# Two images take turns in the 256-state scan, and their block products are made source by source

## The chip, the cores and the metric

The kernel runs on one core of a Trainium2 chip, in one launch. The metric is the device time of an execution in microseconds. Everything is 32-bit floating point. The engines are named as the profile names them: PE is TensorE (PEld its weight loads), DVE is VectorE, ACT is ScalarE, POOL is GpSimd, SP is SyncE, which issues the transfers.

## What is computed

The input is four images of 128 channels and 64 x 64 pixels, that is 4096 positions each. A first layer orders 4 x 4 patches by a score, runs a 16-state scan over them and puts the result back. The second layer, where the change lies, has a selective scan with 256 states and then a long convolution. Cut to what matters, for one image (t is 4096 x 128, normalised before each of the two steps; z, gate and weights as in the code):

```python
# 256-state scan: two halves of 128 inner channels, 256 states
xs, z = split(norm(t) @ W_in)
delta, Bv, Cv = xs @ W_delta, xs @ W_B, xs @ W_C
state = exp(delta[i] * A) * state + delta[i] * Bv[i] * xs[i]      # for every position i
y[i] = sum_n state[:, n] * Cv[i, n]
t = t + (y * silu(z)) @ W_out
# spectral step: 16 causal filters phi over the whole length, with weights M for plus and minus,
# four branches over the first 1, 1/2, 1/4, 1/8 of the positions, plus three taps M_u
t = t + sum_k causal_conv(phi[:, k], norm(t)) @ M[k] + ...
```

The convolution is causal: output positions of a block of 1024 need all earlier blocks and the block itself, of which only the lower triangle.

## The kernel before, in words

`layer0_front` and `layer0_scan` do the first layer; the change doesn't touch them. `layer1` does the second, with an order written out by hand: instructions stand on each engine as the program issues them.

**The scan.** An image is cut into eight chunks of 512 positions (`TS`, `NCH`). A part is one chunk of one image; `parts` (L1207) lists the 32 parts, all chunks of image 0, then of image 1, and so on. A part has 256 steps `k`, and each step does one row d of 2 x 512 elements: `fetch` (L1126, eight steps ahead, two rows at once) loads delta to all partitions, `spread` (L1140, POOL, line L1143, four steps ahead) multiplies it with u, `lift` (L1150, ACT, L1152, one step ahead) makes the decay factors, `scan` (L1154, DVE, L1155) runs the recurrence. After eight steps `contract` (L1160) multiplies the states with c on PE (L1172), copies the products out (L1178), writes them to memory and keeps the last state of every row in `last`, which `carry` (L1132, POOL) adds to the next chunk's first column. A single `last` and a single two-column `halo` serve all images, since chunks of an image follow one another.

**Beside the scan.** `beside` runs, in pieces between the steps, `output` of the part just finished (L916: loads of x2 and gate, gating, output product, normalisation, a token tile for the spectral step, the three-tap product at L973, sum, store to x3) and `project` of the part to come (L809). After each second chunk `output` calls `block`, which queues block products of the spectral step.

**The spectral step.** A task is an image `b`, an output block `blk` of 1024 positions (512 even and 512 odd ones, `r`), and a list of source blocks. It runs 2 x 16 x 2 repetitions (r, filter k, side). A repetition makes, for each source, four products of 128 x 128 tokens with 512 columns of a strip of the filter (L1103; where source and block are the same, with 512, 384, 256 and 128 columns), copies the sum out on ACT (L1114), and multiplies it with the filter's weights `pq` into `fin` (L1047). `load` (L1006) issues the transfers of a repetition, `pq` (L1014, four buffers) and `strip` (L1020, three buffers), three queue entries ahead. Images 0 to 2 get one task for each block with all its sources. Image 3 gets tasks for single sources as these come ready; their sums go to memory as `partial` and are added later through an identity product (L1055). `products` yields the columns of each product, and the main loop takes from it as many columns a step as its pace allows: 1.4 x 512 columns for parts below 20, 1.7 x 512 from there (L1275). What is not taken by the last step, and what the last chunk's output still queues, is issued after the loop by `go_on`, until eight calls in a row gave nothing.

Of the kernel before, what the change touches and what calls it, by code (L numbers as in the profile page):

```python
# [701 lines left out]
def layer1_weights(nc, pool, w_in, w_delta, w_b, w_c, w_out, a_t):  # L702
# [3 lines left out]
    wc = pool.tile([128, 2, 256], F32, name="wc")  # L706
    for t, s in ((wbd[:, :, 0:256], w_b), (wbd[:, :, 256:512], w_delta), (wc, w_c)):
        nc.sync.dma_start(t, s.rearrange("(k p) n -> p k n", p=128))
# [4 lines left out]
    return win, wbd, wc, wo, at  # L713
# [3 lines left out]
def layer1(ctx: ExitStack, tc, ident, half, weights, phi, pqd, mud, x, omd, permd, x2, x3, out):  # L717
# [29 lines left out]
    ones = wp.tile([128, 128], F32, name="ones")  # L747
    nc.vector.memset(ones, 1.0)
# [8 lines left out]
    halo = wp.tile([128, 2], F32, name="halo")  # L757
    last = wp.tile([128, 2, 256], F32, name="last")
# [7 lines left out]
    def small():  # L766
        return sm.tile([128, TS], F32, tag="t2", name="t2")
# [31 lines left out]
    def tiles():  # L799
# [5 lines left out]
            big.tile([128, 2, 256], F32, tag="af", name="af"),  # L805
# [3 lines left out]
    def project(b, ch, into):  # L809
# [39 lines left out]
        for j in range(2):  # L849
# [5 lines left out]
            nc.vector.tensor_tensor(u[:, j, :], ps, xs[:, j, :], ALU.mult)  # L855
        for j in range(2):
            yield "mm"
            ps = middle()
            for k in range(2):
                nc.tensor.matmul(ps, wc[:, k, bass.ts(j, 128)], xs[:, k, :], start=k == 0, stop=k == 1)  # L860
# [13 lines left out]
            d0 = sm.tile([128, 128], F32, tag="d0", name="d0", bufs=1)  # L874
            nc.scalar.activation(d0, ident, AF.Copy, scale=dl[:, 0:1])
            yield "mm"
            ps = middle()
            nc.tensor.matmul(ps[:, 0:128], ones, d0, start=True, stop=True)
# [8 lines left out]
    def put_back():  # L887
# [3 lines left out]
        for h in range(2):  # L891
            for oy in range(4):
# [3 lines left out]
                perm = sm.tile([128, 2, 128], F32, tag="mu", name="perm", bufs=1)  # L896
# [19 lines left out]
    def output(b, ch, yt, gate):  # L916
# [32 lines left out]
        if ch % 2 == 0:  # L949
            tokens[b, ch // 2] = sp.tile([128, 2, 4, 128], F32, tag="tok", name="tok", bufs=5)  # L950
# [9 lines left out]
        mu = sm.tile([128, 3, 128], F32, tag="mu", name="mu", bufs=1)  # L960
        nc.sync.dma_start(mu, mud[:, (0, 1, 2, 2, 3, 3, 3, 3)[ch]])
        yield "post"
        ut = sm.tile([128, 2 + TS], F32, tag="ut", name="ut", bufs=1)
        nc.scalar.copy(ut[:, 2:].rearrange("p (a q) -> p q a", q=2), up.rearrange("p (q a) -> p q a", q=2))
        if ch:
            nc.scalar.copy(ut[:, 0:2], halo)
        else:
            nc.scalar.activation(ut[:, 0:2], ident[:, 0:2], AF.Copy, scale=0.0)
        nc.scalar.copy(halo, ut[:, TS:])
# [7 lines left out]
        if ch % 2:  # L977
            block(b, ch // 2)
# [8 lines left out]
    partial = dr.tile([4, 2, 128, TS], F32, name="partial", bufs=1)  # L987

    def block(b, blk):


        if b < NB - 1:
            tasks = [(b, blk, range(blk + 1), False, True)]
        else:
# [5 lines left out]
            )[blk]  # L1000
        for task in tasks:
            queue.extend(
                (task, r, k, side, src) for r in range(2) for k in range(NK) for side in range(2) for src in task[2]
            )

    def load(i):  # L1006
# [3 lines left out]
        (b, blk, sources, _, _), r, k, side, src = queue[i]  # L1010
        if src == sources[0]:
# [11 lines left out]
    def products():  # L1023
# [6 lines left out]
        def finish(item):  # L1030
            nonlocal fin, xo, sofar
            (b, blk, _, partly, full), r, k, side, pq, u = item
# [4 lines left out]
            cost = TS  # L1037
# [8 lines left out]
            for n, (c0, w) in enumerate([(0, 256), (256, 256)] if blk == 0 else [(0, 512)]):  # L1046
# [4 lines left out]
            if partly and (k, side) == (NK - 1, 0):  # L1051
                sofar = sp.tile([128, TS], F32, tag="conved", name="sofar")
                nc.sync.dma_start(sofar, partial[blk, r])
# [3 lines left out]
            if end:  # L1057
                f, o = fin, xo

                def add():  # L1060
# [5 lines left out]
                    else:  # L1066
                        t = sp.tile([128, TS], F32, tag="conved", name="sum")
                        nc.scalar.copy(t, f)  # L1068
                        nc.sync.dma_start(partial[blk, r], t)
# [4 lines left out]
        while True:  # L1074
# [18 lines left out]
            task, r, k, side, src = queue[i]  # L1093
            b, blk, sources = task[:3]
            if src == sources[0]:
# [4 lines left out]
            for j in range(4):  # L1100
# [4 lines left out]
                    start=src == sources[0] and j == 0, stop=src == sources[-1] and j == 3,  # L1105
                )
                if j < 3:
                    yield TS - skip
            i += 1
            if src == sources[-1]:  # L1110
                u = sp.tile([128, TS], F32, tag="conved", name="conved")

                def empty(u=u, ps=ps):
                    nc.scalar.copy(u, ps)  # L1114
# [17 lines left out]
    def carry(ch, d, ready):  # L1132

        af, vf = ready[4:]
        cols = bass.ds(d, 128)
# [24 lines left out]
    def contract(s, c, g, keep):  # L1160
# [20 lines left out]
        def carried():  # L1181
            if keep:
# [190 lines left out]
```

## Time and profile before

| | |
|---|---|
| median of three runs | 21742.6 us (21742.6 to 21744.73) |
| the profiled execution, its own time | 21746.66 us |
| its span, first to last instruction | 21744.9 us |
| granted PE clock, mean | 0.903 |
| PE busy | 17469.3 us (80%) |
| DVE busy | 20628.6 us (95%) |
| ACT busy | 15865.3 us (73%) |
| POOL busy | 20221.1 us (93%) |
| spread, POOL L1143 | 4096 x 4536 ns |
| scan, DVE L1155 | 8192 x 2272 ns |
| transfers | 4245.65 MB, mean 195 GB/s |

Times of instructions come from the one profiled execution. Busy time is a share of the whole span, and says nothing of which stage an engine holds up; for that the span has to be cut into stages. A matmul in 32 bits shows as two passes, so counts of PE in the profile are twice the program's.

### The profile page before, as it was taken

What the parts mean: (1) busy time and instruction counts of PE and PEld (TensorE: products, weight loads), DVE (VectorE), ACT (ScalarE), POOL (GpSimd) and SP (SyncE); (2) the same over time, 40 slices, a digit from 0 to 9 for tenths busy, and PEclk for the clock granted to TensorE, in tenths of its full rate; (3) what the DMA queues carried; (4) which work ended last, traced back from release to release, by engine and by line L of the source; (5) the groups of instructions that cost most, each with busy time, mean ns of one, the idle gap of its engine ahead of it and who ended that gap; (6) DMA issues with size and microseconds to landing.
All of it is one profiled execution on the core that took longest, in us unless ns stands there. A gap on an engine that the chain in (4) does not pass through costs nothing.

```text
span 21744.9 us, 291339 instructions
## 1 busy us (share of the span) xinstructions
PE 17469.3 (80%) x98516; PEld 7646.0 (35%) x98516; DVE 20628.6 (95%) x11808; ACT 15865.3 (73%) x29216; POOL 20221.1 (93%) x5679
## 2 busy tenths in 40 slices
PE   6788854565858888877768888869498899999999
PEld 3344421222323333333323333324143344434344
DVE  6788889999999999999999999999999999999993
ACT  3677767777777777777777777777777777877773
POOL 2677789999999999999999999999999999999993
PEclk7999966776979999998879999979699999999999
DMA  1455544555757777766667777757476777777775
GB/s 68 112 139 141 140 149 151 173 178 163 217 171 219 219 222 220 218 205 196 201 189 218 222 218 220 222 183 231 154 235 216 226 235 235 234 232 231 232 227 150
DMA packets 2420940, 4245.65 MB, mean 195 GB/s; under 512 B 795208, under 2 KB 1255024, under 8 KB 2416368
## 3 DMA queue, kind: packets, MB, share of 16 engines
q1 hardware_dynamic: 2419440, 4227.01, 63.6%
q8 instruction: 776, 12.71, 0.2%
q14 instruction: 724, 5.93, 0.1%
HBM read 3605.76 MB, written 620.24 MB: 194 GB/s over the span
## 4 chain that ended last, share of the span: by engine, by line
DVE 51%; POOL 23%; PE 9%; ACT 8%; issue 6%; DMA 2%; SPq 0%; DVEq 0%; POOLq 0%; ACTq 0%
DVE s L1155 44%; POOL v L1143 22%; ACT da L1152 5%; PE conv L1103 4%; DVE states L513 3%; DVE p L517 1%; PE yp L1172 1%; ACT f L505 1%; PE fin L1047 1%; PE y L529 1%; DMA dlb<-delta 1%; PE mm L422 1%; DMA yd<-ye 1%; PE conv L104 0%; DVE sum L106 0%
## 5 line engine op out<-in xcount | busy, mean ns | idle before, releaser
L1143 POOL TENSOR_TENSOR v<-u,dlb 128x2044 f32<-128x2044 f32 x4096 | 18333.8, 4536 | 68.1 <-DMA dlb<-delta 64.9
L1155 DVE TENSOR_TENSOR_SCAN s<-da,v 128x1024 f32<-128x1024 f32 x8192 | 18130.6, 2272 | 192.7 <-ACT da L1152 91.1
L1152 ACT ACTIVATE da<-dlb,at 128x511 f32<-128x511 f32 x16384 | 11302.4, 690 | 2235.1 <-DVE s L1155 1774.2
L1103 PE MATMUL conv<-strip,tok 128*128 128x512 f32 (+3 forms) x20480 | 8609.0, 550 | 5.9 <-DMA strip<-in_phi 5.8
L1172 PE MATMUL yp<-s,c 128*32 128x256 f32 x65536 | 5030.9, 438 | 3065.5 <-DVE s L1155 1601.6
L1103 PEld LDWEIGHTS conv<-strip,tok 128*128 128x128 f32 x20480 | 3666.5, 191 | 4104.4 <-issue 3705.1
L1172 PEld LDWEIGHTS yp<-s,c 128*32 128x32 f32 x65536 | 1992.5, 121 | 6865.7 <-issue 1822.2
L1147 ACT COPY v<-vf 128x4 f32<-128x4 f32 x4096 | 812.7, 198 | 2234.0 <-DVE s L1155 2228.7
L491 POOL TENSOR_TENSOR v<-dx,bcb 128x1024 f32<-128x1024 f32 x512 | 1207.2, 2358 | 433.6 <-DVE states L513 427.3
L1047 PE MATMUL fin<-conved,pq 128*128 128x512 f32 (+1 forms) x3200 | 1411.8, 536 | 11.1 <-ACT sum L1068 4.1
L513 DVE TENSOR_TENSOR_SCAN states<-f,v 128x1024 f32<-128x1024 f32 x512 | 1175.9, 2297 | 176.1 <-ACT f L505 126.5
L505 ACT ACTIVATE f<-dt,an 128x255 f32<-128x255 f32 x2048 | 973.6, 476 | 420.0 <-DVE states L513 369.2
L1178 ACT COPY ye<-yp 128x512 f32<-128x512 f32 x2048 | 1185.0, 579 | 16.7 <-PE yp L1172 15.4
L529 PE MATMUL y<-p,ident 128*128 128x512 f32 x2048 | 1004.8, 619 | 152.3 <-DVE p L517 147.4
L1114 ACT COPY conved<-conv 128x512 f32<-128x512 f32 x1344 | 778.0, 579 | 327.7 <-PE conv L1103 326.4
L517 DVE TENSOR_TENSOR p<-states,bcb 128x1024 f32<-128x1024 f32 x512 | 627.0, 1225 | 38.2 <-PE y L535 0.4
L529 PEld LDWEIGHTS y<-p,ident 128*128 128x128 f32 x2048 | 368.3, 195 | 684.0 <-issue 356.3
L1047 PEld LDWEIGHTS fin<-conved,pq 128*128 128x128 f32 x3200 | 528.0, 193 | 221.3 <-issue 160.7
L422 PE MATMUL mm<-ow,yg 128*32 128x128 f32 x2048 | 280.5, 296 | 106.8 <-ACT om L426 105.3
L1063 DVE TENSOR_TENSOR xo<-xo,fin 128x512 f32<-128x512 f32 x32 | 21.3, 667 | 306.8 <-PE fin L1055 306.8
L422 PEld LDWEIGHTS mm<-ow,yg 128*32 128x32 f32 x2048 | 235.3, 138 | 212.5 <-ACT om L426 128.4
L356 PE MATMUL mm<-xin,taps 128*128 128x512 f32 x512 | 237.2, 606 | 28.3 <-DVE f L335 14.0
(242 smaller groups left out, 5932.4 us busy)
## 6 DMA issues: line engine op xcount, KB each, us to landing
dlb<-delta SPq DMA_DIRECT2D x4096, 512.0 KB, 4.1
strip<-in_phi SPq DMA_DIRECT2D x1536, 448.0 KB, 4.8
yd<-ye SPq DMA_DIRECT2D x2048, 256.0 KB, 4.1
bcb<-bcd SPq DMA_DIRECT2D x1024, 256.0 KB, 4.2
strip<-in_phi SPq DMA_DIRECT2D x1024, 256.0 KB, 4.4
pq<-pqd SPq DMA_DIRECT2D x1088, 64.0 KB, 3.8
yt<-yd SPq DMA_DIRECT2D x4096, 4.0 KB, 3.4
pq<-pqd SPq DMA_DIRECT2D x256, 128.0 KB, 4.0
```

What stands on the lines that cost most here:

```text
L491: nc.gpsimd.tensor_tensor(v, ready[n][2][:, :, bass.ts(i, SUB)].unsqueeze(1).broadcast_to((128, 2, 2, SUB)), bc[:, 0].unsqueeze(2).broadca ...
L505: nc.scalar.activation(factors[j % 2][:, a, k, 1:], ready[n][1][:, k, SUB * i + 1 : SUB * i + SUB], AF.Exp, scale=an[:, k, 2 * g + a : 2 * ...
L513: nc.vector.tensor_tensor_scan(states.rearrange(flat), factors[j % 2].rearrange(flat), v.rearrange(flat), 0.0, ALU.mult, ALU.add)
L517: nc.vector.tensor_tensor(p, states, bc[:, 1].unsqueeze(2).broadcast_to((128, 2, 2, SUB)), ALU.mult)
L529: nc.tensor.matmul(t.rearrange("p k t -> p (k t)"), ident, p[:, a].rearrange("p k t -> p (k t)"), start=g == 0 and a == 0, stop=False, ski ...
L1047: nc.tensor.matmul(fin[:, bass.ds(c0, w)], pq[:, n, :], u[:, bass.ds(c0, w)], start=begin and n == 0, stop=end and not partly, skip_group_ ...
L1103: nc.tensor.matmul(ps[:, skip:], tok[:, 1 - r if side else r, j, :], strip[:, bass.ds(c0 - lo, TS - skip)], start=src == sources[0] and j ...
L1143: nc.gpsimd.tensor_tensor(v[:, :, :, 1:], ready[0][:, :, 1:].unsqueeze(1).broadcast_to((128, VD, 2, TS - 1)), dl[:, :, 1:].unsqueeze(2).br ...
L1152: nc.scalar.activation(da[:, h, 1:], dl[:, d % VD, 1:], AF.Exp, scale=at[:, h, d : d + 1])
L1155: nc.vector.tensor_tensor_scan(s[:, d % GD].rearrange("p h t -> p (h t)"), da.rearrange("p h t -> p (h t)"), v[:, d % VD].rearrange("p h t ...
L1172: nc.tensor.matmul(yp[i // 2][bass.ts(q, 32), i % 2], c[:, h, t], s[:, :, h, t], start=h == 0, stop=h == 1)
L1178: nc.scalar.copy(ye, yp[j].rearrange("p i d t -> p i t d"))
```

## The change

Images 0 and 1 are done as before. Then `parts` takes chunk 0 of image 2, chunk 0 of image 3, chunk 1 of image 2, and so on to chunk 7 of image 3. For this `last` and `halo` exist twice, chosen by `b % 2`, and so does `partial`.

Both images' block products are now queued source by source, as image 3's were. The last block's own source of image 3 is split in two: after chunk 6 a task with the token groups 0 and 1 (columns 512 and 384), after chunk 7 a task with groups 2 and 3 (columns 256 and 128), whose copies and closing products take only the last 256 columns. A task's sources are now pairs of a source and its groups. The pace is 1.7 x 512 from part 16.

To make room, W_C is no longer kept in the core's memory but loaded by every `project`; the three-tap weights, their input `ut`, the permutation and W_C share the buffers of the small tiles, three in place of two; `af` has one buffer in place of two; there are six token tiles in place of five. The first delta of a chunk is spread over the partitions by a product with a broadcast column in place of a diagonal tile made on ACT. The loop at the end waits for 16 empty calls in place of eight.

```diff
-    halo = wp.tile([128, 2], F32, name="halo")
-    last = wp.tile([128, 2, 256], F32, name="last")
+    halos = [wp.tile([128, 2], F32, name=f"halo{i}") for i in range(2)]
+    lasts = [wp.tile([128, 2, 256], F32, name=f"last{i}") for i in range(2)]
...
-        return sm.tile([128, TS], F32, tag="t2", name="t2")
+        return sm.tile([128, 2 + TS], F32, tag="t2", name="t2", bufs=3)[:, 0:TS]
...
-            big.tile([128, 2, 256], F32, tag="af", name="af"),
+            big.tile([128, 2, 256], F32, tag="af", name="af", bufs=1),
...
+        wcs = small().rearrange("p (k n) -> p k n", k=2)
+        nc.sync.dma_start(wcs, wc)
...
-            d0 = sm.tile([128, 128], F32, tag="d0", name="d0", bufs=1)
-            nc.scalar.activation(d0, ident, AF.Copy, scale=dl[:, 0:1])
...
-            nc.tensor.matmul(ps[:, 0:128], ones, d0, start=True, stop=True)
+            nc.tensor.matmul(ps[:, 0:128], dl[:, 0:1].broadcast_to((128, 128)), ident, start=True, stop=True)
...
-        mu = sm.tile([128, 3, 128], F32, tag="mu", name="mu", bufs=1)
+        mu = small()[:, 0:384].rearrange("p (i c) -> p i c", i=3)
...
-        if ch % 2:
+        if (b, ch) == (NB - 1, NCH - 2):
+            add([(b, 3, [(3, range(2))], True, False)])
+        elif (b, ch) == (NB - 1, NCH - 1):
+            add([(b, 3, [(3, range(2, 4))], True, True)])
+        elif ch % 2:
             block(b, ch // 2)
...
-        if b < NB - 1:
+        if b < NB - 2:
             tasks = [(b, blk, range(blk + 1), False, True)]
...
-            for n, (c0, w) in enumerate([(0, 256), (256, 256)] if blk == 0 else [(0, 512)]):
+            for n, (c0, w) in enumerate([(0, 256), (256, 256)] if blk == 0 else [(first, TS - first)]):
...
-            for j in range(4):
+            for j in js:
...
-                    nc.scalar.copy(u, ps)
+                def empty(u=u, ps=ps, cols=cols):
+                    nc.scalar.copy(u[:, cols], ps[:, cols])
...
-    parts = [(b, ch) for b in range(NB) for ch in range(NCH)]
+    parts = [(b, ch) for b in range(NB - 2) for ch in range(NCH)]
+    parts += [(b, ch) for ch in range(NCH) for b in (NB - 2, NB - 1)]
...
-        pace = 1.4 if n < 5 * NCH // 2 else 1.7
+        pace = 1.4 if n < 2 * NCH else 1.7
...
-    while idle < 8:
+    idle = 0
+    while idle < 16:
         go_on()
```

## The prediction, made before the result

> **What bounds the kernel now.** I read the page first (the 40 slices), then the 256-state scan cut into its 32 equal parts, then the end of the timeline, then the transfers of that end. All sums are made against the profiled execution: span 21744.9 us, time 21746.7 us, about 4 us above the median of 21742.6 us.
>
> The slices of the page:
>
> ```profile
> PE   6788854565858888877768888869498899999999
> DVE  6788889999999999999999999999999999999993
> POOL 2677789999999999999999999999999999999993
> PEclk7999966776979999998879999979699999999999
> ```
>
> From the sixth slice on VectorE and GpSimd are full, and only in the last one do both fall to 3 while TensorE stays at 9. So there are two regimes: a long one set by scan and spread, and a short end that TensorE has alone. The scan runs from 2863.2 to 21376.7 us. Cut into 32 parts of 578.5 us, one chunk of one image each (columns: stretch and its length, then PE, PEld, DVE, ACT, POOL busy with counts, clock, DMA share, GB/s):
>
> ```profile
> core 0: us, PE busy (x) PEld busy (x) DVE busy (x) ACT busy (x) POOL busy (x), PEclk, DMA share, GB/s
> 4598.80:5177.40 578.60, 264.05 (x2136) 105.48 (x2132) 574.00 (x284) 420.53 (x775) 578.29 (x137) 0.62 0.48 151
> 6334.50:6913.00 578.50, 433.68 (x2687) 177.18 (x2678) 571.94 (x282) 428.88 (x793) 576.31 (x136) 0.86 0.65 200
> 17905.40:18484.00 578.60, 554.47 (x3303) 270.22 (x3304) 570.43 (x285) 451.57 (x841) 577.28 (x137) 1.00 0.77 236
> 20219.60:20798.20 578.60, 553.13 (x2992) 219.46 (x2992) 571.70 (x283) 461.48 (x862) 578.29 (x137) 1.00 0.75 232
> ```
>
> GpSimd is busy for 576 to 578 of 578.5 us in each. TensorE between 264 and 554 us, DMA between 48% and 77%: the length of the part doesn't move with either. The end, in the timeline:
>
> ```profile
> 21374.41 2.26 DVE L1155 TENSOR_TENSOR_SCAN s<-da,v 128x1024 f32<-128x1024 f32 x1
> ...
> 21386.32 0.43 SPq L923 DMA_DIRECT2D t<-gate  x1
> ...
> 21390.63 0.69 DVE L930 TENSOR_TENSOR t<-mm,t 128x512 f32<-128x512 f32 x1 [13.96 <-DMA t<-gate]
> ...
> 21741.22 0.34 SPq L1065 DMA_DIRECT2D out<-xo  x1
> ```
>
> The last scan ends at 21376.7 us, the span at 21744.9: **an end of 368.2 us**, in which TensorE is busy for 358 us (the same view over that stretch). Counted in the order of the TensorE queue, behind the last scan's products stand 210,432 columns (393 convolution, 100 closing matmuls and a few others). The steady state of its last task, the first repetition and the start of the second:
>
> ```profile
> 21601.84 2.32 PE L1103 MATMUL conv<-strip,tok 128*128 128x512 f32 x8
> ...
> 21602.03 0.32 SPq L1014 DMA_DIRECT2D pq<-pqd  x1
> ...
> 21602.40 0.42 SPq L1020 DMA_DIRECT2D strip<-in_phi  x1
> ...
> 21603.99 1.02 PE L1047 MATMUL fin<-conved,pq 128*128 128x512 f32 x2
> ...
> 21604.86 2.32 PE L1103 MATMUL conv<-strip,tok 128*128 128x512 f32 x8
> ```
>
> 3.02 us for 512+384+256+128+512 = 1792 columns, 1.685 ns a column, with no hole. 210,432 x 1.685 = 355 us, plus some 13 us of edges, is the end. The transfers in it (21545 to 21745 us; the three columns of the queue are packets, MB, share):
>
> ```profile
> q1 hardware_dynamic: 18539, 22.14, 42.9%
> ...
> strip<-in_phi SPq DMA_DIRECT2D x61, 256.0 KB, 3.5
> pq<-pqd SPq DMA_DIRECT2D x61, 64.0 KB, 1.8
> ```
>
> A strip lands 3.5 us after its issue (3.1 to 4.4), and here that is hidden, since three are in flight and three repetitions last 9 us.
>
> **The change, part by part.**
>
> *The tail's work.* Counted in the order of the changed program, 47,104 columns stand behind the last scan's products: 64 repetitions of 256+128 convolution and 256 closing columns (40,960), 1,024 of partial sums and 5,120 of the chunk's own output. Nothing else is left: the half task queued one part earlier and all of image 2 end 32 steps before the last scan. So 163,328 columns, 275 us at the rate above, leave the end. That would be the gain if TensorE set the new end. It doesn't.
>
> *What is late next: the strips.* A repetition now has 640 columns, 1.08 us, while its two loads are the same (256 KB, of which only 256 of 512 columns are read, and 64 KB). There are three strip buffers; the load for repetition i+2 waits for the closing matmul of i-2, which stands right behind convolution i-1 (its pq load, ahead of it in the same queue, has four buffers). The circle over three repetitions: convolution 384 x 1.685 = 0.65, closing 0.43, 0.19 to the issue of pq and 0.37 more to that of the strip (the fence above), landing 3.5, about 0.1 to start: 5.25 us, 1.75 us each. DMA: 0.33 MB in 1.75 us is 187 GB/s; the row gives 111 GB/s at 42.9%, so some 260 GB/s if full, 1.27 us each: not the bound, but it may stretch the landing to what it is for such strips under load (4.3 us from 10000 to 11000 us): 2.0 us.
>
> *The clock.* The Trainium skill (TensorE: Matmul & The Clock Gate, Part 1: The HAM clock gate) says that the array falls to half rate only after an idle window of about 3.4 us and is else at full rate. Holes of 0.7 us would then cost nothing: 1.75 us. The rows are less kind: the part with TensorE busy for 264 of 578 us was granted 0.62, and that with 434 of 578 us (75%) 0.86; the new tail is busy for 60%. At half rate the 1.08 us double, and it is 6.3/3 = 2.1 us. I take 1.88 us, near the rule but with a little of both losses: 63 x 1.88 = 118 us; ends 110 and 132 (101 if every strip lands in 3.1 us).
>
> *The way from the last scan to the first of these.* Before, the gate lands 13.9 us after the last scan. From there, taking only durations and leaving out the waits behind queued work: gating and transposes 2.6, output product and sum 2.8, transposes, copy, statistics 2.9, GpSimd and normalisation 3.7, flip and copy 2.0, transposes and copy 1.7, the three-tap product 2.9, sum 0.7: 33 us after the scan; then the store's issue and the pq and strip issues (0.8), and a landing of 3.5 to 4: 38 us. In the last part the spectral queue is empty for those 32 steps, so TensorE is cold as in the parts with scan products alone, where the same lines take 3.78 us for 1.88 (L934), 5.1 for 2.8 (L973), 3.64 for 1.93 (each of two groups of L1172): up to 10 us more. I take 44 us.
>
> *Close.* From the start of the last convolution to the end of the span before: 9.5 us (21735.4 to 21744.9); now 1.1 us of convolution and 0.4 of closing less: 8. Between the two halves of the task one sum and a wait for the single accumulator: 2.
>
> New end: 44 + 118 + 2 + 8 = **172 us** against 368: **196 us less**.
>
> *What is added under the scan.* Parts 16 to 31 get 349,184 columns more: 163,328 from the end, and 185,856 new (image 2 by sources closes 320 times more, the split 64 times, 12 more partial sums), 313 us of TensorE. No part's count goes over 237,824 columns; parts 26 to 30 of before held 237,312 to 237,568 and ran their 578.6 us, and the third row above (part 26, 596 matmuls) is as dense in instructions as any new part. So zero, as long as TensorE stays under the part's length; cover gone, it costs what it overruns. ScalarE: some 25 more copies a part, 0.58 us each, 15 us on 462 of 578. DMA: 384 more pq loads of 64 to 128 KB and a weight load of 256 KB each chunk: under 4 MB a part on 134; the parts at 75 to 77% show no loss. From below no gain is possible: GpSimd is full. From above: parts with full TensorE are 1 to 1.5 us longer than light ones (578.7 against 577.2 between scan starts), and 8 parts change sides: at most 10 us. I take 0 and keep 10.
>
> *Waits that are added.* The load of W_C, the taps and the permutation now take turns with the chunk's small tiles (three buffers in place of two); they stand in SP's queue, and behind them are the delta loads that GpSimd waits for. Delta is fetched eight steps ahead and spread four steps later, 9 us, against a landing of 4.6. At each of these places the old tenant's last reader is at least one group of eight steps back (18 us), so 0; a full miss would cost one spread, 4.5 us, a few times. The factor tile with one buffer: its last reader is GpSimd at step 118, the next writer comes near step 200: 0. One small ScalarE instruction per half chunk goes: off the path. States and halos per image: the carried state is now a part old: 0. The ordering of images 0 and 1 is unchanged.
>
> **Rivals.**
> 1. *TensorE sets the new tail.* If strips land early enough, 63 x 1.08 = 68 us: end 38+68+10 = 116, time about 21490 us. For it: the present tail has no hole. Against: three buffers over a landing of at least 3.1 us give 1.6 us.
> 2. *The strips are later or the clock lower, and the scan loses the few us kept above.* 48 + 132 + 4 + 8 = 192, and 10: about 21576 us.
> 3. *Slower: TensorE becomes the bound of parts 16 to 31.* SP's load for a repetition waits for TensorE (166 us of SP waits for the closing matmul already stand in the last six parts), the delta loads stand behind it, GpSimd behind these. It decides from the point at which a part's TensorE work passes 578.5 us; the densest now take 553 to 556. If the new mix took 600, 14 parts would lose 22 us, 301 in all: 21742.6 - 196 + 301 = 21848 us. Against: the same column count with 596 matmuls fitted.
> 4. *Work is left at the end after all.* The count of the program's order excludes it.
>
> **How the numbers follow.** Likeliest: 21742.6 - 196 = 21547 us, its own range 21522 to 21567. Chances: this case 0.79, rival 1 0.06, rival 2 0.10, rival 3 0.03, a loss in the scan that eats most of the gain 0.02. A measurement of this kernel can tell about 0.2%, 43 us, from no change; so faster 0.95, same 0.02, slower 0.03. The range from 21515 to 21583 takes in rival 2 and the earliest landing; rival 1 and the scan's losses stay out.
>
> **What would show it.** After: last scan again at about 21377 us; no part of the scan over 580 us; first convolution of the last task some 44 us later; repetitions of 1.75 to 2.1 us in which TensorE waits for strips, 1.08 if rival 1 holds; clock in the tail between 0.7 and 1; GpSimd waits for delta grown only if rival 3 holds. I am wrong if the scan's end moves by over 10 us, or if the strips' circle isn't what paces the tail.

## The result, and the profile after

The changed kernel takes 21605.9 us, the median of four runs (21600.6 to 21610.8), against 21743.7 us for the kernel before in the same series (21742.6 to 21745.3). The ratio is 0.9936 with a 95% interval of 0.9924 to 0.9947. That is 138 us less where 196 were forecast, and 23 us above the top of the range. The profiled execution of the changed kernel took 21607.9 us, its span 21606.2 us.

The slices of its page (40 equal parts of the span, busy share in tenths):

```profile
PE   6788854564858888886858999599999999999997
...
POOL 2677789999999999999999999999999999999996
```

The last slice is now mostly scan: GpSimd's last digit is 6 where it was 3, and TensorE's is 7, no longer 9. The end has become short, and TensorE doesn't fill it. The next view cuts the changed kernel at the starts of its scans (columns as before: stretch, its length, busy time of each engine with counts, clock, DMA share, GB/s). The rows are parts 3, 26 and 31, the way from the last scan to the last task, and the last task:

```profile
core 0: us, PE busy (x) PEld busy (x) DVE busy (x) ACT busy (x) POOL busy (x), PEclk, DMA share, GB/s
4595.70:5174.00 578.30, 261.99 (x2120) 104.36 (x2120) 573.09 (x283) 418.91 (x771) 577.99 (x137) 0.62 0.47 152
17937.20:18517.90 580.70, 554.51 (x3166) 245.79 (x3170) 573.30 (x284) 447.08 (x831) 580.39 (x137) 1.00 0.75 230
...
20840.30:21432.20 591.90, 519.71 (x3095) 236.93 (x3093) 570.06 (x271) 461.10 (x839) 573.03 (x131) 0.95 0.72 216
21432.20:21472.00 39.80, 20.05 (x92) 8.30 (x92) 3.90 (x12) 5.26 (x13) 1.21 (x2) 0.61 0.12 39
21472.00:21606.20 134.20, 90.95 (x388) 63.92 (x388) 1.38 (x2) 23.81 (x64) 0.00 (x0) 0.94 0.68 171
```

Two things stand here. GpSimd still fills parts 3 and 26, but part 3 lasts 578.3 us where the same chunk of the same image lasted 577.2 before (between the same scan starts), with TensorE at 262 us and the DMA at 47%: a light part, which the new order doesn't touch, has become longer. And in part 31 GpSimd is not full: 573.0 of 591.9 us.

The balance of the two spans, from the starts of the scans in both traces (us):

| | before | after | difference |
|---|---|---|---|
| first scan starts | 2863.2 | 2858.9 | -4.3 |
| parts 0 to 15 (images 0 and 1) | 9255.7 | 9273.8 | +18.1 |
| parts 16 to 30 | 8681.7 | 8707.5 | +25.8 |
| part 31, to the start of its last scan | 573.8 | 589.6 | +15.8 |
| the whole scan, to the last one's end | 18513.5 | 18573.2 | +59.7 |
| end: last scan to end of span | 368.2 | 174.0 | -194.2 |
| span | 21744.9 | 21606.2 | -138.7 |

Where the text gives the length of part 31 it is measured like this, to the start of its last scan, which is 2.3 us short of its end. The end of 174.0 us is 2 us from the forecast of 172. All that is missing was given back under the scan, where the forecast had put nothing.

**The end.** The timeline of the changed kernel from the last scan on (start, duration, engine, line, out<-in, and in brackets the idle time ahead and its releaser):

```profile
21448.09 0.69 DVE L927 TENSOR_TENSOR t<-mm,t 128x512 f32<-128x512 f32 x1 [15.93 <-DMA t<-gate]
...
21450.73 3.78 PE L931 MATMUL mm<-t,wo 128*128 128x512 f32 x4 [0.78 <-DVE t L927]
...
21472.47 0.44 SPq L1027 DMA_DIRECT2D strip<-in_phi  x1
...
21476.52 1.65 PE L1113 MATMUL conv<-strip,tok 128*128 128x256 f32 x4 [5.64 <-DMA strip<-in_phi]
```

The gate lands 15.9 us behind the last scan's end (21432.2), 2 us later than before. The output product takes 3.78 us, as in a light part. The first strip is issued 40.3 us behind the last scan, and the first convolution starts 44.4 us behind it. A repetition in the steady state of the last task, and the start of the next:

```profile
21500.40 0.42 SPq L1027 DMA_DIRECT2D strip<-in_phi  x1
21500.42 0.89 PE L1113 MATMUL conv<-strip,tok 128*128 128x256 f32 x4 [0.42 <-DMA strip<-in_phi]
21501.15 0.60 PE L1055 MATMUL fin<-conved,pq 128*128 128x256 f32 x2
...
21502.14 0.89 PE L1113 MATMUL conv<-strip,tok 128*128 128x256 f32 x4 [0.40 <-DMA strip<-in_phi]
```

Both convolutions wait for their strip; in the old end's steady state none did. Over the whole last task TensorE waits for a strip 48 times in 64 convolutions, 37.9 us in all, and SP in its turn waits 58 times, 60.7 us in all, until a closing matmul (L1055) lets it issue the next `pq` (L1021), with the strip behind it. From the first to the last of the 64 convolutions 122.1 us pass, 1.94 us a repetition. The transfers of that stretch (21480 to 21600 us: the queue's packets, MB and share; then the size of a strip load and the median time from its issue to its landing):

```profile
q1 hardware_dynamic: 17789, 20.86, 68.8%
...
strip<-in_phi SPq DMA_DIRECT2D x60, 256.0 KB, 3.6
```

A strip still lands 3.6 us after its issue, now at 69% of the DMA and not 43%.

**The scan.** The row of the spread on the pages, of the kernel before and then of the changed one (busy time, mean ns of one, idle time ahead of it on its engine and what ended most of that):

```profile
L1143 POOL TENSOR_TENSOR v<-u,dlb 128x2044 f32<-128x2044 f32 x4096 | 18333.8, 4536 | 68.1 <-DMA dlb<-delta 64.9
```

```profile
L1155 POOL TENSOR_TENSOR v<-u,dlb 128x2044 f32<-128x2044 f32 x4096 | 18381.6, 4552 | 78.1 <-DMA dlb<-delta 68.3
```

As many spreads with the same shapes are busy for 47.8 us more, and GpSimd stands idle ahead of them for 10.0 us more: 57.8 of the 59.7 us. Waiting for delta grew by 3.4 us. (Neighbouring spreads overlap by some 60 ns in the records, so 4096 times the mean is more than the busy time; the busy column and the lengths of the parts are what to compare.)

The added idle time comes in the last part: 14.2 us ahead of its spreads, where the last part of the kernel before had none. Its waits of over a microsecond, in the timeline of the changed kernel, hang together:

```profile
20994.76 0.43 SPq L1027 DMA_DIRECT2D strip<-in_phi  x1
...
20999.16 3.26 PE L1113 MATMUL conv<-strip,tok 128*128 128x512 f32 x4 [3.12 <-DMA strip<-in_phi]
...
21002.46 0.59 ACT L1125 COPY conved<-conv 128x512 f32<-128x512 f32 x1 [4.12 <-PE conv L1113]
...
21004.49 4.47 DVE L1167 TENSOR_TENSOR_SCAN s<-da,v 128x1024 f32<-128x1024 f32 x2 [3.51 <-ACT da L1164]
```

A strip is issued at 20994.76 us and lands 4.4 us later (the median of that part is 4.4), and TensorE has waited 3.1 us for it. ScalarE stands at the copy of that convolution, with the decay factors of the scan behind it in its queue, and is 4.1 us late. VectorE waits 3.5 us for the factors. The late convolution is also slow: 3.26 us, where the same products at 20988.75 us took 1.67. The clock granted from 20998.8 to 21002.2 us was 0.50; it fell so after four of the part's waits for strips.

### The profile page after: what moved, and what is told of

It reads as the page before. It is cut to its first block, busy times and chain, and to the rows that moved or that the text cites. A ratio compares the mean times of both kernels' runs of the same rounds, so it can differ in the third digit from the quotient of the medians.

```text
span 21606.2 us, 294251 instructions
## 1 busy us (share of the span) xinstructions
PE 17698.4 (82%) x99308; PEld 7770.7 (36%) x99308; DVE 20631.8 (95%) x11807; ACT 16015.2 (74%) x29548; POOL 20268.9 (94%) x5679
## 4 chain that ended last, share of the span: by engine, by line
DVE 47%; POOL 22%; PE 13%; ACT 8%; issue 6%; DMA 3%; SPq 0%; DVEq 0%; POOLq 0%; ACTq 0%
DVE s L1167 40%; POOL v L1155 21%; PE conv L1113 5%; ACT da L1164 5%; DVE states L513 3%; PE yp L1184 2%; DVE p L517 1%; PE fin L1055 1%; ACT f L505 1%; DMA dlb<-delta 1%; PE y L529 1%; DMA strip<-in_phi 1%; PE mm L422 1%; DMA yd<-ye 0%; PE conv L104 0%
## 5 line engine op out<-in xcount | busy, mean ns | idle before, releaser
L1155 POOL TENSOR_TENSOR v<-u,dlb 128x2044 f32<-128x2044 f32 x4096 | 18381.6, 4552 | 78.1 <-DMA dlb<-delta 68.3
L1184 PE MATMUL yp<-s,c 128*32 128x256 f32 x65536 | 4952.4, 431 | 2709.5 <-DVE s L1167 1432.2
L1055 PE MATMUL fin<-conved,pq 128*128 128x512 f32 (+1 forms) x3968 | 1799.7, 546 | 16.2 <-ACT sum L1076 8.9
L1125 ACT COPY conved<-conv 128x512 f32<-128x512 f32 (+1 forms) x1728 | 986.6, 571 | 213.8 <-PE conv L1113 212.1
L1055 PEld LDWEIGHTS fin<-conved,pq 128*128 128x128 f32 x3968 | 669.8, 194 | 394.8 <-issue 284.0
L356 PE MATMUL mm<-xin,taps 128*128 128x512 f32 x512 | 237.6, 608 | 27.2 <-issue 13.8
L398 POOL TENSOR_TENSOR e<-e,e 128x1024 f32<-128x1024 f32 x32 | 75.1, 2346 | 186.3 <-DMA bcb<-bcd 150.6
```

The source lines that it names most:

```text
L1055: nc.tensor.matmul(fin[:, bass.ds(c0, w)], pq[:, n, :], u[:, bass.ds(c0, w)], start=begin and n == 0, stop=end and not partly, skip_group_ ...
L1125: nc.scalar.copy(u[:, cols], ps[:, cols])
L1155: nc.gpsimd.tensor_tensor(v[:, :, :, 1:], ready[0][:, :, 1:].unsqueeze(1).broadcast_to((128, VD, 2, TS - 1)), dl[:, :, 1:].unsqueeze(2).br ...
L1184: nc.tensor.matmul(yp[i // 2][bass.ts(q, 32), i % 2], c[:, h, t], s[:, :, h, t], start=h == 0, stop=h == 1)
```

## The experiments

The times of a round were taken on one chip with runs of the kernel before beside them. Each kernel below ran once, `a_best` four times. The lengths of parts come from the trace of each run; parts 0 to 15 are those of images 0 and 1, which both kernels order alike.

### Does the absolute place of the tiles slow the spread; what does the last part's pace cost; what paces the tail?

Parts 0 to 15 became longer though nothing in their order changed, so the first theory was the place of tiles in memory: the new memory plan has u start at byte 31072 of a partition and not at 31552. Two kernels shift everything: the kernel before by 32 bytes, the changed one by 480 (u is back at 31552). The rival is contention from new transfers. A third kernel lowers the pace in the last part only, a fourth halves the strip loads in the last task, of which only the columns used are then loaded.

`b_pad32`, the kernel before with

```diff
+    shift = wp.tile([128, 8], F32, name="shift")
+    nc.vector.memset(shift, 0.0)
```

> The kernel before, with one unused tile of 32 bytes a partition ahead of the second layer's tiles, and nothing else: every later tile stands 32 bytes further on. In the changed kernel even the parts of images 0 and 1, whose work is the same, take 1.2 us longer each, and the mean spread went from 4536 to 4552 ns. Theory 'place': that comes from where the tiles stand (u, delta and v change places modulo 64 bytes against each other and the start), so this kernel's parts grow by about 1.2 us each, the spread's mean to about 4550 ns, the time to about 21743 + 38 = 21780 us. Theory 'work': it comes from what the change adds (loads of W_C, shared buffers, more traffic), so this kernel stays at 21743 us and 4536 ns.

Measured: 21748.9 us beside 21750.2; parts 0 to 15 9255.2 us, spread busy 18333.5. Nothing moved.

`a_pad480`, the changed kernel with the same two lines and `[128, 120]`.

> The changed kernel with an unused tile of 480 bytes a partition, which puts u at the very address that it had before, and delta and v at the same place modulo 64 bytes as before. Theory 'place': the spread's mean returns to about 4536 ns, parts 0 to 15 to their lengths before, the time to about 21606 - 38 = 21568 us. Theory 'work': no change, 21600 to 21611 us and 4552 ns.

Measured: 21605.8 us; parts 0 to 15 9275.2 us, spread busy 18380.3. Nothing moved either. A shift of all the layer's tiles together is not the cause, and the theory in this form fell.

`a_pace`, the changed kernel with

```diff
-        pace = 1.4 if n < 2 * NCH else 1.7
+        pace = 1.4 if n < 2 * NCH else 1.7 if n < 31 else 1.55
```

> The changed kernel with a pace of 1.55 x 512 columns a step in place of 1.7 in the last part alone; the queue is then just empty at the last scan. In the changed kernel the last part takes 589.6 us against 573.8 before, with TensorE waiting for strips and ScalarE and VectorE behind it around step 62 to 94. If that is the half task's short repetitions asking for strips faster than SP and three buffers bring them, a lower pace spreads them: the last part at 575 to 580 us, time about 21595 us. If it is something that the pace does not set (the loads of y in the same queue, or the output of the chunk before), the last part stays at 586 to 590 us and the time at 21606 us.

Measured: 21603.9 us. The last part took 577.5 us, 12.1 less than with the change as it was. In this run parts 0 to 15 took 5.4 us more than in the trace of the changed kernel, which hides nearly half of it in the total: that fell by 2 us against the median of the changed kernel, where 11 were expected. The part came out as expected (575 to 580). The waits of the last part, first in the kernel before, then in the changed kernel, then in `a_pace` (who waits for whom: us in total, times, longest us):

```profile
ACT conved L1114 <- PE conv L1103: 3.9, 6, 1.2
...
DVE s L1155 <- ACT da L1152: 1.1, 2, 0.7
...
PE conv L1103 <- DMA strip<-in_phi: 0.2, 1, 0.2
```

```profile
ACT conved L1125 <- PE conv L1113: 29.6, 19, 4.1
DVE s L1167 <- ACT da L1164: 21.0, 17, 3.5
...
PE conv L1113 <- DMA strip<-in_phi: 12.4, 8, 3.1
```

```profile
ACT conved L1125 <- PE conv L1113: 9.5, 10, 4.2
PE conv L1113 <- DMA strip<-in_phi: 7.9, 7, 2.3
DVE s L1167 <- ACT da L1164: 7.1, 4, 3.9
```

The chain strip, convolution, copy, factors, scan shrinks in all its links: VectorE's wait for the factors falls by 13.9 us and the part by 12.1. The half task has only 512+384+512 = 1408 columns for each pair of loads, and asks for a pair every 3.66 us (median from convolution to convolution), where the own-source tasks with 1792 columns do so every 4.32 us, in either kernel. The part issued 122 strip loads of 256 KB, the last part of the kernel before 105 (64 of 256 KB and 41 of 448 KB). But the number of loads alone does not do it: `a_pace` brings 123 through its last part. And TensorE's waits for strips fall only from 12.4 to 7.9 us, while ScalarE's waits behind TensorE fall from 29.6 to 9.5. So the lower pace may help as much by the room that it leaves TensorE to catch up as by earlier strips; the two were not separated.

`a_narrow`, the changed kernel with

```diff
-        width = 896 if src < blk else 512
+        width = 896 if src < blk else 512 - 128 * sources[which][1][0]
```

> The changed kernel with the last half task's strips loaded only as wide as they are read, 256 columns (128 KB) in place of 512. In the tail a repetition takes 1.93 us, against 1.08 us of products. If the circle of three strip buffers and the landing paces it, a smaller strip lands about 0.6 to 0.8 us earlier and a repetition takes 1.65 to 1.75 us: 12 to 18 us less, time about 21591 us. If the issue of the two loads or the products of a cold TensorE pace it, nothing changes: 21606 us.

Measured: 21601.8 us, the end 165.5 us, 1.81 us a repetition in place of 1.94: 8 us, less than expected. A strip of half the bytes lands after 3.3 us, not 3.6. So the landing hardly follows the bytes, and TensorE still waits for 48 of the 64 strips.

### Memory plan or order?

The second theory: not where the tiles lie, but how far the spread's inputs lie from each other. In the kernel before, the delta tile lies 41440 bytes behind u in each partition, in the changed one 37408. The rival: the new order with its transfers and TensorE work. `b_mem` has the new memory plan (and its W_C loads) with the old order; `a_gap` has the new order and restores only the distance.

`b_mem`, the changed kernel with

```diff
-    parts = [(b, ch) for b in range(NB - 2) for ch in range(NCH)]
-    parts += [(b, ch) for ch in range(NCH) for b in (NB - 2, NB - 1)]
+    parts = [(b, ch) for b in range(NB) for ch in range(NCH)]
...
-        if b < NB - 2:
+        if b < NB - 1:
...
-        if (b, ch) == (NB - 1, NCH - 2):
-            add([(b, 3, [(3, range(2))], True, False)])
-        elif (b, ch) == (NB - 1, NCH - 1):
-            add([(b, 3, [(3, range(2, 4))], True, True)])
-        elif ch % 2:
+        if ch % 2:
...
-        pace = 1.4 if n < 2 * NCH else 1.7
+        pace = 1.4 if n < 5 * NCH // 2 else 1.7
```

> The changed kernel with the order, the tasks, the split and the pace of before put back: what is left of the change is its memory plan alone (W_C loaded by each chunk, small tiles in three shared buffers, one factor tile, six token tiles, two sets of carried states, the broadcast product). Theory 'work, of the memory plan': the 1.2 us a part come from here, so every part of this kernel is 1.2 us longer than before and the spread's mean 4550 ns: about 21780 us. Theory 'order': parts 0 to 15 and all others as before, 4536 ns, about 21745 to 21750 us.

Measured: 21786.4 us beside 21742.8. The scan lasts 18556.2 us, 42.7 more than before: parts 0 to 15 +20.9, parts 16 to 30 +20.5, part 31 +1.3. Its spread row:

```profile
L1151 POOL TENSOR_TENSOR v<-u,dlb 128x2044 f32<-128x2044 f32 x4096 | 18377.1, 4549 | 65.4 <-DMA dlb<-delta 64.2
```

43.3 us more busy time and no more idle time than before. So the memory plan alone costs about 43 us, evenly in all parts (1.3 us each), and it costs them in the spreads themselves, not in a wait: with the weight loads in SP's queue GpSimd waits no longer for delta than before (64.2 and 64.9 us).

`a_gap`, the changed kernel with

```diff
-    lasts = [wp.tile([128, 2, 256], F32, name=f"last{i}") for i in range(2)]
...
+    lasts = [sm.tile([128, 2, 256], F32, name=f"last{i}", bufs=1) for i in range(2)]
...
-        rs = sm.tile([128, NT], F32, tag="rs", name="rs")
+        rs = sp.tile([128, NT], F32, tag="rs", name="rs", bufs=2)
```

> The changed kernel with the carried states and one small tile placed elsewhere, so that the distance from u to delta and v in a partition is what it was before, 41440 bytes in place of 37408; nothing else. Shifting everything together did nothing, and kept this distance. Theory 'distance': the spread's mean goes back to 4536 ns and the parts by 1.2 us each, 21606 - 38 = 21568 us. Theory 'work': 4550 ns and 21600 to 21611 us.

Measured: 21573.4 us beside 21742.8. Parts 0 to 15 9258.5 us (15.3 less than the changed kernel), parts 16 to 30 8687.2 (20.3 less), part 31 589.4 (the same), the end 174.8.

```profile
L1156 POOL TENSOR_TENSOR v<-u,dlb 128x2044 f32<-128x2044 f32 x4096 | 18339.9, 4536 | 83.5 <-DMA dlb<-delta 66.9
```

The spread's busy time is back to 6.1 us over that before. The carried states and one small tile in other places, with the same loads, products and order, are worth 36 us of the scan. What is left in parts 16 to 30, 5.5 us over before, would be the order's (`b_mem` gives 25.8 - 20.5 = 5.3 by the other way); but single runs with the same distance scatter by as much, and `a_best` has 2.9.

`a_whole`, the changed kernel with the last block's own source in one task, queued after the last chunk:

```diff
-        if (b, ch) == (NB - 1, NCH - 2):
-            add([(b, 3, [(3, range(2))], True, False)])
-        elif (b, ch) == (NB - 1, NCH - 1):
-            add([(b, 3, [(3, range(2, 4))], True, True)])
-        elif ch % 2:
+        if ch % 2:
```

> The changed kernel with the last block's own source in one task after the last chunk, not in two halves. If the sums of the prediction hold: a repetition in the tail is 1792 columns, 3.02 us, with its strips hidden; tail 44 + 63 x 3.02 + 10 = 244 us in place of 174. The last part loses the half task, and with it the stalls: 575 us in place of 590. Together 21606 + 70 - 14 = 21662 us. If the last part's stalls are not the half task's, it stays near 588 us: 21675 us.

Measured: 21669.2 us, between the two totals; the part decides. The end lasts 248.4 us (repetitions of 195.1/63 = 3.10 us), and part 31 575.8. So the split is worth 74.4 us in the end and gives back 13.8 in the last part: 60.6 of the 138 us. In this form it is the half task that makes part 31 long, at its pace.

`a_pairs`, the changed kernel with both sides of a filter in one strip transfer of 2 x 256 columns and one `pq` transfer, so that three buffers hold six repetitions:

```diff
-        src = sources[which][0]
+        src, js = sources[which]
+        if js[0]:
+            if side == 0:
+                pq = sp.tile([128, 2, 128], F32, tag="pq", name="pq", bufs=4)
+                nc.sync.dma_start(pq, pqd[k, :, :, 3].rearrange("s p e -> p s e"))
+                strip = sp.tile([128, 896], F32, tag="strip", name="strip")
+                both = strip[:, 0:512].rearrange("p (s c) -> p s c", s=2)
+                apart = NK * row + r - 1
+                nc.sync.dma_start(both, bass.AP(phi.tensor, k * row + 1, [[1, 128], [apart, 2], [1, 256]]))
+                for s in range(2):
+                    mats[i + s] = pq[:, s : s + 1]
+                    strips[i + s] = both[:, s], 0
+            return
...
-            while issued < len(queue) and issued < i + 3:
+            while issued < len(queue) and issued < i + (5 if queue[issued][0][2][0][1][0] else 3):
```

> The changed kernel with the last half task's loads made for two repetitions at once: one strip load of 2 x 256 columns, one load of both weights, so that three strip buffers hold six repetitions. If the circle of buffers and landing paces the tail (5.8 us over three repetitions, 1.93 each), over six it is under the 1.08 us of products, and TensorE sets the tail: 63 x 1.1 = 70 us in place of 122, time about 21554 us. If the loads' own time or SP's issue sets it, a repetition stays above 1.5 us: over 21578 us.

Measured: 21592.2 us, the end 141.3 us, 85.1 us from first to last convolution, 1.35 us a repetition. Two neighbouring repetitions in its timeline, and its strip loads from 21500 to 21580 us:

```profile
21510.18 0.82 PE L1125 MATMUL conv<-strip,tok 128*128 128x256 f32 x4
21510.83 0.60 PE L1067 MATMUL fin<-conved,pq 128*128 128x256 f32 x2
21511.27 0.82 PE L1125 MATMUL conv<-strip,tok 128*128 128x256 f32 x4
```

```profile
strip<-in_phi SPq DMA_DIRECT2D x29, 256.0 KB, 5.3
```

Most repetitions now take 1.09 us with no wait (640 columns at 1.70 ns), though the strip lands later, after 5.3 us. TensorE nearly sets this end. That shows that the circle of buffers and landing set the changed kernel's: half the bytes alone left 1.81 us (`a_narrow`), and the issues, of which this kernel has half as many, took SP some 0.75 of 1.94 us (0.32 for `pq`, 0.42 for the strip). Which buffers was not separated: in the changed kernel SP's waits stand at `pq` with its four buffers, ahead of the strip with its three, and no run gave `pq` a fifth. The expected total was missed by some 38 us for other reasons: a wait for strips remains every few repetitions, the way to the first convolution is 48.3 us, and part 31 (594.1) and parts 0 to 15 (9280.0) came out long.

### Is it the distance of the inputs, and what law does it follow?

`a_gap64` leaves out the second half of the edit of `a_gap` (`rs` stays where the change has it), which puts delta 41504 bytes behind u, 64 more than before. `a_gapv` is `a_gap` with 64 bytes between delta and the product tile v, so that the inputs keep their distance, while v and all tiles behind it (the states, the strips, the tokens) move away from both:

```diff
+    apart = []
...
+        if not apart:
+            apart.append(wk.tile([128, 16], F32, name="apart", bufs=1))
+            nc.vector.memset(apart[0], 0.0)
```

> As the run that restored the distance from u to delta (41440 bytes, 21573 us, spread 4536 ns), but 64 bytes more: 41504. The distance of the changed kernel, 37408, leaves the same remainder in steps of 4096, 2048 and 1024 bytes as 41504. Theory 'remainder': the spread is slow again, 4550 ns, about 21608 us. Theory 'far apart' (some 4 KB more are what helps): it stays at 4536 ns and 21573 us.

> As the run that restored the distance from u to delta, with 64 bytes more between delta and v, so that u to delta stays 41440 and delta to v becomes 16448 in place of 16384 (v and the states keep their distance). If the two inputs u and delta matter, the spread stays at 4536 ns and the time at 21573 us. If the output's place against an input matters, the spread is slow again, 4550 ns, about 21608 us.

Measured: `a_gap64` 21609.0 us with parts 0 to 15 at 9280.2 and 18386.8 us of spread; `a_gapv` 21565.1 us with 9259.7 and 18342.2 (both beside 21745.4). 64 bytes more between u and delta cost the whole sum, 64 bytes between delta and v cost nothing. 41504 and 37408 bytes, 4096 apart, give the same busy time, as theory 'remainder' has it.

Three more distances, `a_gapp32`, `a_gapp96` and `a_gapp128`: `a_gap` with 32, 96 and 128 bytes between u and delta, by (n = 32, 96, 128)

```diff
+    apart = sm.tile([128, n // 4], F32, name="apart", bufs=1)
+    nc.vector.memset(apart, 0.0)
```

> The run with the restored distance (41440 bytes from u to delta), with 32 bytes more: 41472, a multiple of 64 and of 128. So far 41440 was fast (spread 4536 ns) and 41504 and 37408 slow (4548 to 4552). Theory 'steps of 128': only the remainder by 128 counts, 96 for the fast one and 32 for the slow ones; 41472 has 0 and lies beyond both, so its spread is another value, and if nearness decides it is between them or as slow, 4540 to 4555 ns, parts 0 to 15 together 9256 to 9285 us. Theory 'smaller is faster': it depends on the distance itself, and 32 bytes on from 41440 it is halfway, 4543 ns, 9269 us.

> The same with 96 bytes more: 41536, remainder 64 by 128, 0 by 64. Theory 'steps of 128': a value of its own, equal to that of 41472 if steps of 64 were enough, but 41440 and 41504 have shown that they are not. Theory 'the distance itself': slow, 4550 ns or more, parts 0 to 15 9280 us.

> The same with 128 bytes more: 41568, remainder 96 by 128 as with the fast 41440. Theory 'steps of 128': fast again, 4536 ns, parts 0 to 15 together 9258 us, time 21565 to 21573 us. Theory 'the distance itself' or a longer step: slow, 4550 ns, 9280 us, 21607 us.

Measured: 21582.3, 21602.6 and 21587.4 us beside 21741.3. All distances together:

| bytes from u to delta | kernels | parts 0 to 15, us | spread busy, us |
|---|---|---|---|
| 41440 | before, `b_pad32`, `a_gap`, `a_gapv`, `a_best` | 9255.2 to 9259.7 | 18333.5 to 18342.2 |
| 41472 | `a_gapp32` | 9263.4 | 18354.8 |
| 41504 | `a_gap64` | 9280.2 | 18386.8 |
| 41536 | `a_gapp96` | 9273.8 | 18376.0 |
| 41568 | `a_gapp128` | 9269.6 | 18366.5 |
| 37408 | after, `b_mem`, `a_pad480`, `a_pace`, `a_narrow`, `a_whole`, `a_pairs` | 9273.8 to 9280.0 | 18377.1 to 18387.0 |

Within one distance the runs scatter by 5 to 10 us; the first line and the last don't come near each other. It is neither a step (against `a_gap`, 32 bytes cost 15 us of spread, 64 cost 47) nor a line (128 cost 27). The four middle lines are one run each, and 15 us is not far beyond the scatter. Which law it is stays open. It also stays open whether u is the tile that counts: in all these kernels the tiles next to u moved with it. That it is the distance of u and delta is inferred from these two being the spread's inputs; shown is only that moving the tiles around delta and v against those around u does it, and that moving everything, or v with the tiles behind it, doesn't.

### All of it together

`a_best` is the changed kernel with `a_gap`, `a_pairs` and the last part's pace of 1.55, and it queues the last half task before the last chunk's output, so that its first strips are loaded while the output is made; its products are held back until then:

```diff
+    held = [False]
...
+        if (b, ch) == (NB - 1, NCH - 1):
+            held[0] = True
+            add([(b, 3, [(3, range(2, 4))], True, True)])
...
-            add([(b, 3, [(3, range(2, 4))], True, True)])
+            held[0] = False
...
+            if held[0] and queue[i][0][2][0][1][0]:
+                yield 0
+                continue
```

> The changed kernel with what the runs point to, together: the distance from u to delta as before (35 us), a pace of 1.55 in the last part (12 us), the last task's loads made for two repetitions at once (33 us in the tail), and the first of them issued before the last chunk's output and not after it (some 5 us, since the first strip then waits for nothing). If the four add up: 21606 - 85 = 21521 us. If the tail then loses again what it gained, because the early loads delay those of the output, 21530 us.

Measured: 21518.3 us (21517.2 to 21521.8) against 21745.4 for the kernel before (21740.3 to 21752.7), ratio 0.9896 with an interval of 0.988 to 0.9913. The scan lasts 18519.1 us (5.6 over before), part 31 575.6, the first convolution comes 38.2 us after the last scan, the end is 136.9 us. It is 88 us below the changed kernel: by the two traces 54.1 in the scan and 37.1 in the end, 91.5 us of the spans in all. From the first to the last convolution 90.8 us pass, 5.7 more than in `a_pairs`, so part of what the early loads win is lost again.

## Why the prediction failed, point by point

- **The tail's work and what paces the new tail: right.** Forecast 44 + 118 + 2 + 8 = 172 us; measured 44.4 to the first convolution, 122.1 to the last (118 and the 2 between the halves), 7.5 behind: 174.0. TensorE waits for strips in 48 of 64 repetitions, as forecast, and the two experiments on it agree: fewer bytes help a little (1.81 us), more repetitions in flight remove most of the wait (1.09 us in most repetitions, 1.35 in the mean). That the sum comes out to 2 us is in part luck: 1.88 us was a middle value between 1.75 and 2.1, not a sum. With the measured landing of 3.6 us the circle gives 1.78; landings between 3.1 and 5.1 us and a few repetitions at half clock bring it to 1.94, in shares that were not separated. Rival 1's end, 116 us, is not reached even by `a_pairs`.
- **The landing: close.** Estimated at 3.5 us up to 4.3 under load; 3.6 measured at 69% of the DMA.
- **The clock: the number was right, the reason was not.** By the rows of parts with idle TensorE the tail would have been granted 0.62 to 0.86; it got 0.94 with TensorE busy for 91 of 134 us. The way to the tail, with long idle stretches, was granted 0.61, and its output product took the forecast 3.78 us. But this trace does not agree with what the Trainium skill says (TensorE: Matmul & The Clock Gate, Part 1: The HAM clock gate), that the low rate comes after an idle window of about 3.4 us. The clock fell to half in the tail too, after much shorter holes:

```profile
21486.83 1.53 PE L1113 MATMUL conv<-strip,tok 128*128 128x256 f32 x4 [0.45 <-DMA strip<-in_phi]
```

  The same products took 0.89 us in the repetition before. The longest hole in the 3.4 us ahead was 1.46 us, TensorE was busy for 1.48 of the 3.4 us, and the next 3.4 us were granted 0.50. What fits the tail and the light parts alike stands in the last section.
- **TensorE in parts 16 to 30: right.** The densest part holds 554.5 us of 580.7; rival 3 did not come. Parts 16 to 30 lost some 5 us to the order at most, inside the "at most 10" that the forecast kept for parts that change sides. (That a part's length doesn't move with TensorE's load could not be read from windows cut to equal lengths; the starts of the scans, 577.2 to 578.7 us apart, do show that it moves little.)
- **The step that failed: what is added under the scan, "I take 0".** The scan became 59.7 us longer. Two terms of it were put at nothing and were not:
  - the memory plan. "Waits that are added" asked of each shared buffer only whether somebody would wait for it. Nobody does (idle time for delta 64.9 and 68.3 us), that answer was right. But the plan also moved the inputs of the spread against each other, and each spread of 4.5 us became about 10 ns longer: 36 us (the changed kernel against `a_gap`) to 43 us (`b_mem` against before) in 4096 of them. The forecast had the bound engine's instruction at its old duration because its line of code wasn't touched.
  - the last part, 14 us (15.8 less the 1.3 of the memory plan). The forecast compared columns and the count of instructions with the densest old part, and these did fit (519.7 us of TensorE). It didn't compare how close the loads follow each other: the half task needs a pair every 3.66 us in place of 4.32, through the same three buffers and the same SP queue, with the same landing of 4.4 us. TensorE waits for strips for 12.4 us in place of 0.2, ScalarE behind it for 29.6 in place of 3.9, and VectorE for the factors for 21.0 in place of 1.1. The forecast worked the strip buffers out for the tail and did not ask for them one part earlier. That the half task at its pace is the cause is shown (`a_whole`, `a_pace`); how much of it is the wait for a buffer, SP's queue, the lower clock after a wait or the lack of slack was not separated.
- The sum: 36 to 43, 14 and some 5 make 55 to 62 of the 59.7 us. The start of the scan, 4.3 us earlier, was not forecast; `b_mem` has it too (2858.5), so it belongs to the memory plan.
- The forecast's own sign of failure, a last scan that moves by more than 10 us, came: 21432.2 for 21376.7.

## What to carry to other kernels

When a change moves tiles in memory, the durations of the bound engine's instructions are no longer those of the old trace, even where their lines are untouched: ask what 0.2% on the commonest instruction would cost, and keep it in the range. A task made of short repetitions needs its loads looked at in every stage in which it runs, and a pace that leaves room for a late one: here copies in ScalarE's queue carried a late strip on to the engine that sets the time. To find where a change under a full engine costs, compare first a stretch that the change doesn't touch.

## What the hardware showed that was not expected

The time of a GpSimd multiplication of two inputs in the core's memory depended on where its tiles lie to each other in a partition: 18334 to 18342 us of busy time for 4096 of them at a distance of 41440 bytes, 18377 to 18387 at 37408 or 41504, values between at three others, and no effect from a shift of everything by 32 or 480 bytes. The landing of a small strip hardly followed its bytes: 3.6 us for 256 KB at a DMA share of 69%, 3.3 us for 128 KB at 55%, but 5.3 us for 256 KB taken as two runs of 256 columns for each partition, at 78%.

The clock followed TensorE's busy share over stretches of 3.41 us, the step in which the trace of the changed kernel records it. From the start of the scan it fell to half 332 times, always after a stretch with TensorE busy for 48% or less; in 248 of them no hole reached 3.4 us. Of the 4169 stretches after which it stayed full, 99% had 49% or more. It came back only after stretches with 76% or more. So the tail, busy for 68%, fell seldom, and the parts busy for 46% were granted 0.62.
